# Biases loaded packed instead of multiplied into place, a longer warming burst, and other batches with a copy, in a convolution-attention kernel

## The chip, the cores and the metric

The kernel runs on one core of one Trainium2 chip. Its engines work side by side, each through its own queue in order: TensorE multiplies matrices (PE in the profile, its weight loads PEld), VectorE (DVE), ScalarE (ACT) and GpSimd (POOL) work elementwise, and the queues of SyncE (SP), ScalarE and GpSimd issue transfers (DMA). Matrix products are written to PSUM, which has eight banks of 512 float32 columns; the other engines read them from there.

The metric is the time of one execution on the device in microseconds (us), as the median of several runs.

## The reference

The input `x` has four images of 384 channels and 48 x 48 pixels, so 2304 tokens of 384 channels each, in float32. Cut to what matters:

```python
x_flat = x.reshape(B, C, N).transpose(0, 2, 1)
local = conv_general_dilated(x, conv_w, padding='SAME', feature_group_count=C)   # 7 x 7, each channel alone
inv = bn_gamma * rsqrt(bn_var + BN_EPS)
local = local * inv + (bn_beta - bn_mean * inv)
x_norm = layernorm(x_flat, ln_gamma, ln_beta)          # over the 384 channels
q, k, v = split_heads(x_norm @ qkv_w.T + qkv_b)        # 8 heads of 48
q = q + split_heads(layernorm(local_flat, ln_gamma, ln_beta))
attn = softmax(q @ k.T * 48 ** -0.5)
out = x_flat + (attn @ v) @ proj_w.T + proj_b
```

## The kernel before, in words

**Layout.** The 384 channels lie in three chunks of 128 partitions, packed so that two heads share 128 partitions: 48 channels of one head, 16 of a shared tail, 48 of the next, 16 of the tail (`segments`). Whatever is per channel must come in this order: the convolution's taps, the norms, the biases.

**Tiles.** An image is cut in six groups of 384 tokens for keys and values (`from_x`) and in five query tiles of 8, 10, 10, 10 and 10 pixel rows, 384 or 480 columns each. For each query tile there are eight batches; a batch scores nine blocks of 128 keys against the tile for one pair of heads (`score`, line 1169), ScalarE takes the exponential (lines 1181 and 1185), and the weighted sums follow (`weigh`, line 1206). Tiles are numbered t = 0 to 19 over the four images.

**The convolution** runs on VectorE as a stream of multiply-adds, one for each tap and chunk (line 376). `convolve_first(n)` takes the next n taps of that stream in the start-up, as written by hand; in the attention a planner (`plan`) deals them out to slots (t, s, q), where s is the batch and q a quarter of it: `spare` says how much VectorE time a slot is thought to have, and each tile's taps have a due slot. Since an engine's queue runs in order, taps dealt before a copy or a norm delay it.

**Copies.** A batch scores into pairs of banks. In a batch for which `eased(t, s)` holds, the second half of its third block is copied by VectorE out of PSUM (line 1189) and ScalarE takes its exponential later from there, so that a bank comes free earlier and ScalarE gets time. In image 0 before its last tile, batches 3, 5 and 6 have the copy, and in tile 3 batch 2 too.

**Start-up.** The order is written by hand, and the same on all engines' queues. TensorE first multiplies constant tiles (`warm`, line 1388). The query and key biases come in natural order with one small load on ScalarE's queue (line 202), a few VectorE writes make a matrix of ones that picks rows (`bias_rows`), and four products put the biases in packed order into `qk_vec` (`bias_out`, lines 297 and 301; float32 products count twice in the profile, so eight entries). The first group of x is then normalized in three blocks: mean of the loaded rows (`slab`), centring on VectorE (line 659), squares on ScalarE (line 598), mean of the squares, inverse root (lines 667 to 669 on ScalarE, 678 and 679 on VectorE), scaling (line 736). In between, `pack` (line 251) puts the taps and norms in order, ScalarE copies them out as `vec` (line 258), and scales the weights by the norm's gain (lines 953, 960, 961). `shift_rows` and `columns` (lines 916 and 942) turn the norm's shift into a bias of keys, values and queries, and `key_bias` and `query_bias` add `qk_vec` to it. Then the loop over groups 1 to 5 makes keys, values and queries of each while the next group is normalized (sums on VectorE at lines 608 and 609, their mean on TensorE at line 649), and `convolve_first` fills VectorE between. `products` (line 451) does one chunk of one tile's taps on TensorE instead. The first score follows at line 1169.

Of the kernel before, what the change touches and what calls it, by code (L numbers as in the profile page):

```python
# [16 lines left out]
P = 128  # L17
NH = 8
HD = 48
# [8 lines left out]
SPLIT = 5  # L28
EASED = 2
X_LATER = 3  # L30
WARM = 9
BIASES_AFTER = 2
SHIFTS = 4
AHEAD = 24
SLAB_AT = 40
# [15 lines left out]
def unshifted_pass(  # L51
# [16 lines left out]
    nc = tc.nc  # L68
# [3 lines left out]
    CC = C // P  # L72
    G = RG * W
    NG = N // G
    NB = G // P
    NP = NH // 2
# [5 lines left out]
    NA = len(ROWS)  # L82
# [30 lines left out]
    def two_banks():  # L113
        nonlocal n_banks
        i = n_banks % 8
        n_banks += 2
        return banks[:, i : i + 2, :]
# [4 lines left out]
    def load_packed(dst, src, queue=nc.sync):  # L122
        for p0, piece in segments(src):
            queue.dma_start(out=dst[p0 : p0 + piece.shape[0]], in_=piece)
# [41 lines left out]
    qk_vec = const.tile([P, 2, CC], F32, tag="qk_vec", name="qk_vec")  # L166
    vbp = const.tile([P, CC, 1], F32, tag="vbp", name="vbp")
    pb = const.tile([P, CC], F32, tag="pb", name="pb")
    ident = const.tile([P, P], F32, tag="ident", name="ident")
# [14 lines left out]
    def piece(*shape):  # L184
        nonlocal taken
        size = 1
        for n in shape:
            size *= n
        part = start_up[:, taken : taken + size]
        taken += size  # L190
        names = "abc"[: len(shape)]
        return part.rearrange(
            f"p ({' '.join(names)}) -> p {' '.join(names)}", **dict(zip(names, shape))
        )
# [3 lines left out]

    of_ln = piece(2, CC)
    nc.scalar.dma_start(out=of_ln, in_=ln)  # L200
    biases = piece(2, NP)
    nc.scalar.dma_start(out=biases[0 : 2 * HD], in_=qk_b.rearrange("j d v p -> (j d) v p"))
    of_values = piece(CC, 1)
    nc.scalar.dma_start(out=pb, in_=proj_b)
    staged = [
# [9 lines left out]
    nc.gpsimd.tensor_scalar_add(inv, norms[:, 3], BN_EPS)  # L215
    nc.gpsimd.tensor_tensor(inv, inv, neg_half, ALU.pow)
    load_packed(of_values, v_b.rearrange("o c -> c o"), nc.gpsimd)

    pieces = []
    for c in range(CC):  # L220
        for r, n, first in ((0, HD, 0), (64, HD, 1), (48, 16, 6), (112, 16, 7)):
            head = first + 2 * c if first < 6 else first
            ch = head * HD + (16 * c if first >= 6 else 0)
            while n:
                part = min(n, P - ch % P)
                pieces.append((c, r, ch // P, ch % P, part))
                r, n, ch = r + part, n - part, ch + part
# [48 lines left out]
            load_slab(0, 1, queue=nc.sync)  # L276
    load_packed(w_o, proj_wT)
    loads.close()

    chosen_rows = spread_taps[1][:, 2 * 448 : 2 * 448 + 4 * P].rearrange("p (a m) -> p a m", m=P)  # L280

    def bias_rows():

        rows = chosen_rows.rearrange("p a (j x) -> p a j x", j=2)
        nc.vector.memset(chosen_rows, 0.0)
        nc.vector.tensor_copy(
            rows[:, 0, :, 0:HD], ident[:, 0 : 2 * HD].rearrange("p (j d) -> p j d", j=2)
        )
        nc.vector.tensor_copy(
            rows[:, 1:4, :, HD:64],  # L290
            ident[:, 0 : 2 * HD].rearrange("p (j c r) -> p c j r", j=2, c=CC),
        )

    def bias_out():
        m = two_banks()[:, 0, 0 : 2 * CC].rearrange("p (v c) -> p v c", v=2)
        rows = slice(0, 2 * HD)
        nc.tensor.matmul(
            m, lhsT=chosen_rows[rows, 0, :], rhs=biases[rows, :, 0:CC], start=True, stop=False
        )
        for c in range(CC):  # L300
            nc.tensor.matmul(
                m[:, :, c],
                lhsT=chosen_rows[rows, 1 + c, :],
                rhs=biases[rows, :, CC],
                start=False,
                stop=c == CC - 1,
            )
        nc.scalar.copy(qk_vec, m)

    taps = sorted(range(KS * KS), key=lambda t: (abs(t // KS - PAD), abs(t % KS - PAD)))
    accs = {}
# [148 lines left out]

    def eased(t, s):
        if t < NA - 1:
            return s in (3, 5, 6) or s == 2 and t == NA - 2
        return s > 0 or t >= NA

    def spare(t, s, q):
# [437 lines left out]
    rows = {}  # L907
# [25 lines left out]
                rows[i][:, 288:384].rearrange("o (h u r) -> o u h r", h=2, r=16),  # L933
            )

    def columns():

        r, r2 = two_banks(), two_banks()
        m = {1: r[:, 0, 0:CC], 2: r[:, 1, 0:CC], 0: r2[:, 0, 0:CC]}
        for i in m:  # L940
            for c in range(CC):
                nc.tensor.matmul(
                    m[i][:, c : c + 1],
                    lhsT=row[of_row(i), c * P : (c + 1) * P],
                    rhs=one[of_row(i)],
                    start=True,
                    stop=True,
                )
        return m, r2[:, 1, :G]

    def scale_values(*chunks):
        for c in chunks:
# [425 lines left out]
    def convolve_first(n):  # L1378
        nonlocal n_first
        n_first += n  # L1380
        for _ in range(n):
            next(stream)


    def warm(n):
        m = two_banks()[:, 0, 0:P]
        for _ in range(n):
            nc.tensor.matmul(m, lhsT=mean_w, rhs=ident, start=True, stop=True)

    bias_rows()  # L1390
    in_order_of_channels()
    warm(WARM - BIASES_AFTER)
    bias_out()
    warm(BIASES_AFTER)

    blocks = [slice(i * P, (i + 1) * P) for i in range(NB)]
    raw = slabs[0, 0][0]
# [24 lines left out]
    next(making)  # L1422
    for c in range(CC):
        scale_rows(0, c)
    m, bank = columns()
    convolve_first(11)
    norm = Norm(xn[0, 1])
    norm.mean_by_chunk(norm.src, bank)
    convolve_first(9)
    key_bias(m)  # L1430
    convolve_first(3)
    query_bias(m)
    next(making)
    norm.centre()
    norm.squares()
    both(making)
    convolve_first(5)
    norm.mean_by_chunk(norm.buf)
    norm.root()
    both(making)  # L1440
# [9 lines left out]
    for g in range(1, NG):  # L1450

        last = g == NG - 1
        making = from_x(0, g)
        if last:
            norm.centre()
            norm.squares()
        both(making)
        if not last:
            norm.mean_in_place()
            convolve_first(6)  # L1460
        if g in (3, 5):
            keep_stack(0, g // 2 - 1)
        if last:
            convolve_first(2)
            norm.sum_squares()
            norm.mean_in_place()
            norm.root()
            convolve_first(4)
        else:
            norm.centre()  # L1470
            norm.squares()
        both(making)
        if not last:
            if g == 1:
                taps_out()
            if g == 2:
                products()
                convolve_first(22)
            convolve_first(3 if g == 1 else 5)
            norm.sum_squares()  # L1480
            both(making)
            norm.mean_in_place()
            norm.root()
        if last:
            local_end(0, norm.newton())
            query_end(0, True)
            low_queries(0, 0, nc.gpsimd)
            lows_out(1)
            both(making)
            convolve_first(5)  # L1490
            lows_out(2)
            convolve_first(4)
            both(making)
            convolve_first(6)
            both(making)
            continue
        lows_out(1)
        both(making)
        convolve_first(6)
        lows_out(2)  # L1500
        norm.scale(norm.newton())
        if g == 1:
            taps_spread()
        both(making)
        if g == NG - 2:
            assert n_first >= each
            norm = Norm(accs[0])
            norm.mean_by_chunk(norm.src)
        if g < NG - 2:
            norm = Norm(xn[0, g + 2])  # L1510
            norm.sum()
        convolve_first((7, 5, 6, 6)[g - 1])
    made = n_first - each
    plan(made)
    convolve("start")
# [1 line left out]
    for t in range(NT):  # L1517
        b, g = divmod(t, NA)
        if g == 0 and b:
# [4 lines left out]
            norm = None  # L1524
# [645 lines left out]
```

## Time and profile before

| | us |
|---|---|
| median of three runs | 2699.64 |
| the three runs | 2699.25, 2699.64, 2702.36 |
| the profiled execution's own time | 2702.91 |
| its span, first to last instruction | 2700.4 |
| TensorE busy in it | 2689.2 |
| VectorE busy | 2352.3 |
| ScalarE busy | 1650.4 |
| GpSimd busy | 595.5 |
| first score starts | 152.0 |

A row of the profile names the engine, the line of the kernel, the operation, what it writes and reads, shapes, and how often. In rows in order of time the first two numbers are the start and the length, both in us from the span's first instruction; a bracket says how long the engine was idle before and what ended that. In the chain of waits each row is a stretch of the chain that ended last. Products are pipelined, so a row's length is more than the time from its start to the next row's start; rates are read from starts.

### The profile page before, as it was taken

The page shows a single profiled execution, that of the slowest core. Times are in us where ns is not written, and L with a number is a line of the kernel's source. Part 1 is how long each engine was busy: PE and PEld are TensorE (multiplying, and loading weights), DVE is VectorE, ACT ScalarE, POOL GpSimd, SP SyncE. Part 2 cuts the span into 40 slices and gives each one's busy share as a digit, 9 for nine tenths or more (in the row PEclk, how much of TensorE's full clock was granted, in tenths as well). Part 3 has the DMA queues.
Part 4 walks back from the last instruction along what each step waited for, and adds up shares of the span by engine and source line. Part 5 has one row for each costly group of instructions (what it writes and reads, how often), then busy time and mean ns, then how long its engine had stood idle before and what let it go on. Part 6 is the DMA issues. An engine that isn't in the chain of part 4 may idle for free.

```text
span 2700.4 us, 45544 instructions
## 1 busy us (share of the span) xinstructions
PE 2689.2 (100%) x16444; PEld 1543.1 (57%) x16444; DVE 2352.3 (87%) x4105; ACT 1650.4 (61%) x2489; POOL 595.5 (22%) x1065
## 2 busy tenths in 40 slices
PE   9999999999999999999999999999999999999999
PEld 6565555555566655555555655555555665555555
DVE  8999999999999999888999999888899899887212
ACT  4367667777325777777622767777753376766662
POOL 4441111112462111011155111101116401101110
PEclk9999999999999999999999999999999999999999
DMA  8454443546465545355456553545636644445442
GB/s 175 88 162 136 133 125 115 143 128 159 113 157 162 147 115 146 115 154 136 126 141 159 158 149 110 151 124 140 149 103 166 167 131 132 139 124 147 136 129 94
DMA packets 160251, 370.43 MB, mean 137 GB/s; under 512 B 58400, under 2 KB 107360, under 8 KB 160016
## 3 DMA queue, kind: packets, MB, share of 16 engines
q0 software_dynamic: 70816, 277.78, 36.2%
q1 hardware_dynamic: 83456, 79.29, 13.1%
q10 hardware_dynamic: 5744, 10.36, 1.2%
q8 instruction: 132, 2.16, 0.3%
q14 instruction: 103, 0.84, 0.1%
HBM read 258.14 MB, written 64.14 MB: 119 GB/s over the span
## 4 chain that ended last, share of the span: by engine, by line
PE 89%; DVE 9%; ACT 1%; issue 0%; DMA 0%; DVEq 0%; ACTq 0%
PE banks L1206 38%; PE banks L1169 31%; PE banks L741 19%; DVE acc L376 7%; PE banks L631 0%; DVE qs L1030 0%; DVE acc L659 0%; DVE pt L852 0%; DMA start_up<-in_qk_b_dram 0%; DVE xn L736 0%; DVE pt L1189 0%; DVE xn L659 0%; DVE sq L678 0%; DVE sq L608 0%; DVE sq L609 0%
## 5 line engine op out<-in xcount | busy, mean ns | idle before, releaser
L376 DVE SCALAR_TENSOR_TENSOR acc<-slab,vec,acc 128x470 f32<-128x470 f32 (+10 forms) x2832 | 1657.1, 657 | 0.0
L1206 PE MATMUL banks<-pt,v 128*64 128x480 f32 (+1 forms) x5760 | 1149.7, 553 | 0.0
L1185 ACT ACTIVATE pt<-banks 128x960 f32<-128x960 f32 (+1 forms) x1140 | 1000.6, 948 | 114.7 <-PE banks L1169 59.8
L1169 PE MATMUL banks<-qs,ks 64*128 64x480 f32 (+1 forms) x8640 | 953.0, 372 | 1.5 <-DVE pt L1189 1.4
L1169 PEld LDWEIGHTS banks<-qs,ks 64*128 64x128 f32 x8640 | 786.3, 184 | 222.2 <-issue 113.9
L1206 PEld LDWEIGHTS banks<-pt,v 128*64 128x64 f32 x5760 | 399.8, 137 | 672.4 <-issue 627.0
L813 POOL DMA_DIRECT2D ks<-wide x220 | 159.8, 726 | 1476.8 <-PE banks L1169 1472.5
L1181 ACT ACTIVATE pt<-banks 128x480 f32<-128x480 f32 (+1 forms) x460 | 263.7, 573 | 119.7 <-PE banks L1206 119.2
L741 PE MATMUL banks<-xn,w_qk 128*128 128x384 f32 x864 | 284.0, 486 | 0.0
L741 PEld LDWEIGHTS banks<-xn,w_qk 128*128 128x128 f32 x864 | 164.0, 190 | 114.7 <-issue 0.7
L1189 DVE COPY pt<-banks 128x480 f32<-128x480 f32 (+1 forms) x140 | 89.1, 637 | 151.9 <-PE banks L1169 150.1
L1054 ACT COPY o<-banks 113x480 f32<-113x480 f32 (+1 forms) x80 | 43.6, 545 | 205.4 <-PE banks L1206 205.4
L741 PE MATMUL banks<-w_v,xn 128*128 128x384 f32 x432 | 145.2, 488 | 0.5 <-ACT w_v L953 0.3
L835 ACT COPY v<-banks 128x384 f32<-128x384 f32 x72 | 34.3, 477 | 156.8 <-PE banks L741 156.8
L1064 ACT COPY ao<-banks 113x480 f32<-113x480 f32 (+1 forms) x60 | 32.7, 545 | 151.2 <-PE banks L1206 151.2
L741 PEld LDWEIGHTS banks<-w_v,xn 128*128 128x128 f32 x432 | 81.3, 190 | 59.2 <-DVE xn L736 1.8
L1073 DVE TENSOR_TENSOR ao<-ao,o 113x480 f32<-113x480 f32 (+1 forms) x60 | 37.9, 632 | 59.4 <-ACT o L1054 59.0
L1181 ACT ACTIVATE pt<-pt 128x480 f32<-128x480 f32 (+1 forms) x140 | 88.4, 632 | 0.0
L741 PE MATMUL banks<-af,w_o 128*128 128x384 f32 (+1 forms) x270 | 85.2, 470 | 0.0
L798 POOL DMA_DIRECT2D wide<-pt x120 | 60.1, 504 | 111.5 <-ACT pt L849 106.8
L741 PEld LDWEIGHTS banks<-af,w_o 128*128 128x128 f32 x270 | 51.3, 190 | 31.9
L849 ACT ACTIVATE pt<-banks,qkb 128x384 fp32r<-128x384 f32 x60 | 34.6, 581 | 56.4 <-PE banks L741 51.1
(160 smaller groups left out, 1455.5 us busy)
## 6 DMA issues: line engine op xcount, KB each, us to landing
ks<-wide POOLq DMA_DIRECT2D x220, 768.0 KB, 5.1
qs<-qs SPq DMA_DIRECT2D x346, 60.0 KB
slab<-in_x_dram POOLq DMA_DIRECT2D x22, 432.0 KB, 6.7
wide<-ks POOLq DMA_DIRECT2D x12, 768.0 KB, 5.2
xr<-in_x_dram POOLq DMA_DIRECT2D x16, 576.0 KB, 5.0
rb<-rden SPq DMA_DIRECT2D x32, 270.0 KB
held<-ao POOLq DMA_DIRECT2D x12, 720.0 KB, 4.5
xn<-in_x_dram POOLq DMA_DIRECT2D x36, 216.0 KB, 5.0
```

Of the source, the lines that this page charges most:

```text
L376: nc.vector.scalar_tensor_tensor(dst, src, weight, dst, ALU.mult, ALU.add)
L741: nc.tensor.matmul(dst, lhsT=weights(c), rhs=src(c), start=c == 0, stop=c == CC - 1)
L798: nc.gpsimd.dma_start(out=last[16 * u : 16 * u + 16, 0], in_=k[r : r + 16, 0])
L813: queue.dma_start(out=place_keys(b, p, i), in_=wide[b, p][:, :, at])
L849: nc.scalar.activation(k[:, 0, :], r[:, :G], AF.Identity, bias=bias)
L1054: nc.scalar.copy(part[0 : 64 + HA], sums[0 : 64 + HA, :n])
L1073: nc.vector.tensor_add(dst, dst, part[0 : 64 + HA])
L1169: nc.tensor.matmul(r[:, j, :n], lhsT=ks[rows, w, at], rhs=qs[rows, m, :], start=n_th == 0, stop=n_th == 2,)
L1181: nc.scalar.activation(weights_of[:, at, :n], src, AF.Exp, scale=SCALE)
L1185: nc.scalar.activation(to, r[:, :, :n], AF.Exp, scale=SCALE)
L1189: nc.vector.tensor_copy(weights_of[:, second, :n], r[:, 1, :n])
L1206: nc.tensor.matmul(sums[halves[j], :n], lhsT=values[t // NA, kb // NB][:, first : first + 64], rhs=weights_of[:, at[j], :n], start=start, ...
```

## The change

The query and key biases are no longer loaded in one piece and multiplied into order. Eight small loads on GpSimd's queue, behind the value bias, write them straight into `qk_vec`: for each of queries and keys one load of the 48-channel parts and three of 16-channel tails, with elements of 12 and 4 bytes. The load on ScalarE's queue, `bias_rows` and `bias_out` go. `WARM` rises from 9 products, which stood in two parts (seven, then two behind the bias products), to 12 in one piece.

In the first group, the mean of the second group of x is issued ahead of `columns`, which now gets its banks from outside. VectorE does 17 taps in one go, then centres that group, and adds the key and query biases after that; before, it did 11, 9 and 3 taps around them and centred last. The 11 taps that follow were 5. In the loop two taps leave group 2 (22 to 20), one is added at the end of groups 3 and 4 each (6 to 7), and in the last group 2 and 4 become 1 and 5; the number of taps in the start-up stays at 176.

In image 0 the copy stays in batches 5 and 6 of tiles 0 and 2, in 3 and 5 of tile 1, and in 2, 3, 5 and 6 of tile 3. Batch 3 of tile 0, batch 6 of tile 1 and batch 3 of tile 2 lose it. Since `spare` asks `eased`, the planner deals the taps out a little differently too.

```diff
-WARM = 9
-BIASES_AFTER = 2
+WARM = 12
...
-    biases = piece(2, NP)
-    nc.scalar.dma_start(out=biases[0 : 2 * HD], in_=qk_b.rearrange("j d v p -> (j d) v p"))
...
     load_packed(of_values, v_b.rearrange("o c -> c o"), nc.gpsimd)
+    for j in range(2):
+        r = 64 * j
+        nc.gpsimd.dma_start(out=qk_vec[r : r + HD], in_=qk_b[j, :, :, 0:CC])
+        for c in range(CC):
+            nc.gpsimd.dma_start(
+                out=qk_vec[r + HD : r + 64, :, c], in_=qk_b[j, 16 * c : 16 * c + 16, :, CC]
+            )
...
-    def bias_rows():
...
-    def bias_out():
...
     def eased(t, s):
         if t < NA - 1:
-            return s in (3, 5, 6) or s == 2 and t == NA - 2
+            return s in ((5, 6), (3, 5), (5, 6), (2, 3, 5, 6))[t]
         return s > 0 or t >= NA
...
-    def columns():
-
-        r, r2 = two_banks(), two_banks()
+    def columns(r, r2):
+
...
-        return m, r2[:, 1, :G]
+        return m
...
-    bias_rows()
     in_order_of_channels()
-    warm(WARM - BIASES_AFTER)
-    bias_out()
-    warm(BIASES_AFTER)
+    warm(WARM)
...
-    m, bank = columns()
-    convolve_first(11)
+    r, r2 = two_banks(), two_banks()
     norm = Norm(xn[0, 1])
-    norm.mean_by_chunk(norm.src, bank)
-    convolve_first(9)
+    norm.mean_by_chunk(norm.src, r2[:, 1, :G])
+    m = columns(r, r2)
+    convolve_first(17)
+    norm.centre()
     key_bias(m)
-    convolve_first(3)
     query_bias(m)
     next(making)
-    norm.centre()
     norm.squares()
     both(making)
-    convolve_first(5)
+    convolve_first(11)
...
         if last:
-            convolve_first(2)
+            convolve_first(1)
             norm.sum_squares()
             norm.mean_in_place()
             norm.root()
-            convolve_first(4)
+            convolve_first(5)
...
             if g == 2:
                 products()
-                convolve_first(22)
+                convolve_first(20)
...
-        convolve_first((7, 5, 6, 6)[g - 1])
+        convolve_first((7, 5, 7, 7)[g - 1])
```

More of the change, by code (lines that the diff above doesn't have):

```diff
@@ L278, in unshifted_pass @@
     loads.close()
-    chosen_rows = spread_taps[1][:, 2 * 448 : 2 * 448 + 4 * P].rearrange("p (a m) -> p a m", m=P)
-    def bias_rows():
[L284 to L292, printed above, removed]
-    def bias_out():
[L295 to L308, printed above, removed]
     taps = sorted(range(KS * KS), key=lambda t: (abs(t // KS - PAD), abs(t % KS - PAD)))
```

## The prediction

> **What bounds the kernel now.** I read the page first, then the engines' rows in order of time for the start-up, the chain of waits, and the rows and windows of the attention. The page's shares say that TensorE (PE) hardly rests:
>
> ```profile
> PE 2689.2 (100%) x16444; PEld 1543.1 (57%) x16444; DVE 2352.3 (87%) x4105; ACT 1650.4 (61%) x2489; POOL 595.5 (22%) x1065
> ```
>
> So only two things can shorten the run: PE time that is spent badly, or short waits of PE. The diff touches the start-up (before the first score, at 152.0) and the planner's copies in image 0. PE's first rows (start, length, both us; each float32 product counts as two entries):
>
> ```profile
> 1.81 3.35 PE L1388 MATMUL banks<-ident,mean_w 128*128 128x128 f32 x14 [1.81 <-POOL one L177]
> 6.01 0.56 PE L297 MATMUL banks<-start_up,spread 96*128 96x6 f32 x2 [0.85 <-DMA start_up<-in_qk_b_dram]
> 6.43 1.42 PE L301 MATMUL banks<-start_up,spread 96*128 96x2 f32 x6
> 7.71 1.20 PE L1388 MATMUL banks<-ident,mean_w 128*128 128x128 f32 x4
> 8.70 4.05 PE L741 MATMUL banks<-slab,mean_w 128*128 128x128 f32 x18
> 12.54 1.23 PE L741 MATMUL banks<-sq,mean_w 128*128 128x128 f32 x6
> 13.61 1.66 PE L251 MATMUL banks<-natural,start_up 128*128 128x52 f32 x14
> 15.11 1.57 PE L741 MATMUL banks<-sq,mean_w 128*128 128x128 f32 x12
> 16.51 1.46 PE L741 MATMUL banks<-w_v,xn 128*128 128x384 f32 x4
> 18.24 3.00 PE L741 MATMUL banks<-w_v,xn 128*128 128x384 f32 x8 [0.28 <-ACT w_v L953]
> ```
>
> Equal entries ran at two rates: (12.54 - 8.70) / 18 = 0.213 us each, then (16.51 - 15.11) / 12 = 0.117. The six at 12.54 took 1.07, so the rate doubled among them, at about 13.3. The windows' granted clock reads 1.00 throughout (as in the window's row below, and the same in the first 20 us), so I take the rate from the starts. The warming burst of 3.35 us broke off at the wait for the query and key biases, and the narrow entries after it did not raise the rate.
>
> In the attention of image 0, scoring a batch of 480 columns takes 6.12 us at best (1130.10); here it takes 6.45, and where VectorE (DVE) must copy one half out, up to 333.11 + 2.22 - 328.33 = 7.00:
>
> ```profile
> 174.55 5.38 PE L1169 MATMUL banks<-qs,ks 64*128 64x384 f32 x54
> 185.82 3.60 PE L1169 MATMUL banks<-qs,ks 64*128 64x384 f32 x37
> 190.25 1.84 PE L1169 MATMUL banks<-qs,ks 64*128 64x384 f32 x17 [0.83 <-DVE pt L1189]
> 209.25 5.03 PE L1169 MATMUL banks<-qs,ks 64*128 64x384 f32 x54
> 328.33 4.38 PE L1169 MATMUL banks<-qs,ks 64*128 64x480 f32 x37
> 333.11 2.22 PE L1169 MATMUL banks<-qs,ks 64*128 64x480 f32 x17 [0.40 <-DVE pt L1189]
> 384.68 6.45 PE L1169 MATMUL banks<-qs,ks 64*128 64x480 f32 x54
> 398.45 4.39 PE L1169 MATMUL banks<-qs,ks 64*128 64x480 f32 x37
> 403.04 2.21 PE L1169 MATMUL banks<-qs,ks 64*128 64x480 f32 x17 [0.20 <-DVE pt L1189]
> 1130.10 6.12 PE L1169 MATMUL banks<-qs,ks 64*128 64x480 f32 x54
> ```
>
> The window of tile 1 (us, then busy us and instructions of PE, weight loads, DVE, ACT, POOL, the clock, transfers):
>
> ```profile
> 245.53:357.15 111.62, 111.22 (x731) 60.05 (x729) 110.08 (x180) 78.11 (x104) 13.84 (x21) 1.00 0.47 128
> ```
>
> The three waits are for that copy, which stands in DVE's queue behind convolution taps; DVE is busy 110.08 of 111.62 us in tile 1.
>
> **The change, part by part.**
>
> *Bias products and warming.* Out go the 0.85 us wait, eight narrow entries (6.01 to 7.71) and three short DVE writes that lie in DVE's idle time; in come six more entries of warming. All 24 then run from 1.81 to 1.81 + 24 x 0.213 + 0.16 = 7.1 at the slow rate. The first means need the slab. Its landing has no row: its four loads are issued by 3.04, the nearest rows for landings are 4.0 and 4.8 us, so 7.0 to 7.8, and 8.7 at the latest, since PE did not wait for it then. I take 7.4 instead of 8.70: -1.3.
>
> ```profile
> 1.19 1.85 SPq L124 DMA_DIRECT2D slab<-in_x_dram  x4
> 3.85 2.44 POOL L124 DMA_DIRECT2D start_up<-in_v_b_dram  x4
> 4.70 6.26 SPq L124 DMA_DIRECT2D staged<-in_qkv_wT_dram  x12
> 15.31 0.29 ACT L258 COPY vec<-banks 128x156 f32<-128x156 f32 x1 [0.36 <-PE banks L251]
> ```
>
> ```profile
> xn<-in_x_dram POOLq DMA_DIRECT2D x36, 72.0 KB, 4.8
> start_up<-in_v_b_dram POOLq DMA_DIRECT2D x2, 0.6 KB, 4.0
> ```
>
> *The rate.* In this run a dense burst of 3.35 us was too short, one of 5.6 us (7.71 to 13.3) long enough. So an unbroken one from 1.81 doubles the rate between 5.2 and 7.4. The 38 entries between 8.70 and 15.11 took 6.41 us; at 0.107 (the 14 of L251, 13.61 to 15.11) to 0.117 they take 4.1 to 4.5. I take 4.5, since the third block's square must still be waited for: -1.9. ScalarE's copy of the packed vectors (15.31) and its scalings up to PE's 18.24 then come 3.2 earlier. The value weights are the first four of twelve loads, issued by about 6.8, so landed by 11.6 with 4.8, and wanted at 12.4, behind that copy. Range of both terms together: -1.3 (no doubling) to -3.6 (slab at 7.0).
>
> [...]
>
> *Eight bias loads on GpSimd (POOL).* They queue behind the value bias: issued from 6.3 at 2.44 / 4 = 0.61 each, done at 11.2, landed by about 15.2. The key bias needs them at about 27.6 and POOL's own next work, writing out keys, follows that. Price nothing; one for one, if they landed after 27.6.
>
> *Mean of the second x first; 17 taps in one go.* The number of PE's products stays. Now PE stands 0.80 at 35.41, because DVE does 23 taps before centring; afterwards it does 17, and 15 follow instead of nine.
>
> ```profile
> 35.41 2.20 PE L741 MATMUL banks<-sq,mean_w 128*128 128x384 f32 x6 [0.80 <-ACT sq L598]
> 87.02 0.88 PE L649 MATMUL banks<-sq,mean_w 128*128 128x384 f32 x2 [0.40 <-DVE sq L609]
> 93.95 4.14 PE L741 MATMUL banks<-w_v,xn 128*128 128x384 f32 x12 [0.24 <-DVE xn L736]
> 137.65 0.88 PE L649 MATMUL banks<-sq,mean_w 128*128 128x384 f32 x2 [0.21 <-DVE sq L609]
> 39.43 0.62 DVE L678 SCALAR_TENSOR_TENSOR sq<-banks,eps,sq 128x384 f32<-128x384 f32 x1 [0.33 <-ACT sq L669]
> 130.10 3.75 DVE L376 SCALAR_TENSOR_TENSOR acc<-slab,vec,acc 128x470 f32<-128x470 f32 x6
> 140.29 0.62 DVE L678 SCALAR_TENSOR_TENSOR sq<-banks,eps,sq 128x384 f32<-128x384 f32 x1 [0.34 <-ACT sq L669]
> 135.15 1.17 ACT L598 ACTIVATE sq<-acc 128x1152 f32<-128x1152 f32 x1 [2.90 <-DVE acc L659]
> ```
>
> ```profile
> 44.15 7.96 DVE acc L376 x16
> 73.36 12.45 DVE acc L376 x27
> ```
>
> That frees PE, but the chain of waits (last two rows) is DVE's from 42 to 94, and the number of taps up to there is the same. DVE gains its 0.33 wait at 39.43 and loses some 0.2 waiting for the moved mean: -0.1. I take that, not the 0.8 that PE alone could save; the lower end of this term is -0.8.
>
> *Taps moved.* Two taps leave the 27 before the sums at 87.02: 2 x 12.45 / 27 = -0.9, which PE's waits 0.40 and 0.24 and what hides in its pipeline can use. They come back one each in groups 3 and 4. The last one costs: seven taps of 0.61 (3.75 / 6) instead of six before the centring of the first query tile, and ScalarE's squares (1.17) are covered by one tap instead of two, so the sums at 137.65 come 0.55 later against PE. A fifth tap (0.6) then stands before the query's root is used at 140.29, where 0.34 was waiting: +0.25. Sum up to the first score: -3.2 - 0.1 - 0.9 + 0.55 + 0.25 = -3.4.
>
> *Copies.* Batch 3 of tile 0, batch 6 of tile 1 and batch 3 of tile 2 lose theirs. They then score like neighbours without one: 5.38 instead of 190.25 + 1.84 - 185.82 = 6.27, so -0.89; 6.45 instead of 7.00, -0.55; 6.45 instead of 6.80, -0.35. DVE gets three copies back, 3 x 0.55 to 0.65, about what PE gains, so its load stays where it is:
>
> ```profile
> L1189 DVE COPY pt<-banks x14: 546/648/658, 189.6 to 595.9; 128x480 f32<-128x480 f32 x11, 128x384 f32<-128x384 f32 x3
> ```
>
> The planner's own sums shift single taps between slots of a tile. Where one moves ahead of a copy that stays, up to 0.6 is lost, where one moves behind it, as much is won: 0. Together -1.8 (-2.4 to -0.6).
>
> Total for the profiled execution: -5.2, from 2702.91 (span 2700.4 and 2.5 around it) to **2697.7**.
>
> **How that stands to the median.** The runs shown are 2699.25, 2699.64 and 2702.36; the profiled one lies by the slowest. Two pairs about 3.2 apart, and one thing in the trace is worth 3.2: when the rate doubles. Had the first burst of 3.35 us sufficed, the means would begin at 7.5 and run at the fast rate: -1.2 - 1.9 = -3.1. I read the two lower runs so; they have that gain already and keep 5.2 - 3.1 = 2.1, which leads from their 2699.45 to 2697.4. Both ways meet near **2697.4**, my forecast. Against the median that is -0.08%: no change, as some 0.2% (5.4 us) is what a measurement of this kernel can tell.
>
> **Rivals.** (a) *The two pairs have another cause* than the rate; one profile cannot say. Then the whole 5.2 comes off the median: 2694.4. (b) *The rate still doubles late*: the pause between 7.1 and 7.4 breaks the burst, and it takes 5.6 us from 7.4. Then 1.3 remains of the 3.2: 2702.6 - 3.3 = 2699.3. Against it: the burst is 5.3 us long before the pause. (c) *The copies buy nothing*: DVE, 98.6% busy, gives PE's gain back at the copies that stay (batches 5 and 6 of tile 0, 3 and 5 of tile 1, 5 and 6 of tile 2): 2697.4 + 1.8 = 2699.2. (d) *Slower*, by the same queue: a late copy costs 6.27 - 5.03 (209.25, where it came in time) = 1.2. If DVE comes some 0.8 too late at all six, they cost 7.2, and 2699.2 + 7.2 = 2706.4; two such copies more than eat the gain. It decides from about 0.5 of delay at each; now only the three that go wait.
>
> **How the numbers follow.** Forecast 0.57 (own range 2696 to 2698.6), (a) 0.2, (b) 0.08, (c) 0.11, (d) 0.04. Of (a), which lies near the bound, and of the forecast's edge about 0.17 is faster by over 0.2%; of (d) 0.04 slower; the rest within. The range 2693.9 to 2699.7 holds all but (d) and the tails.
>
> **What would show it.** Right: slab means from about 7.4 at 0.112 each; the vectors' copy near 12.1; first score near 148.6; scoring of the three batches 5.4, 6.45 and 6.45; no wait for L1189's copy over 0.3. Wrong: means still at 0.213; a first score before 148 (PE bound, not DVE) or after 150; waits at the copies that stay; runs of the new kernel that again lie 3 us apart.

## The result, and the profile after

The changed kernel takes 2697.54 us, the median of 20 runs (2696.77 to 2699.66). Twenty runs of the kernel before, the three that the prediction had among them, have a median of 2701.68 (2699.25 to 2704.26), 2.04 above that of those three alone. The ratio is 0.9985, with an interval of 0.9978 to 0.9992: the gain of 4.1 us can be told from none, and with 0.15% it is within the 0.2% that the prediction calls no change. The profiled execution took 2696.89 us with a span of 2695.0; before, 2702.91 and 2700.4. So the span lost 5.4 us.

Lines of the changed kernel have other numbers: 741 is now 712, 649 is 620, 376 is 347, 1169 is 1139, 1189 is 1159, 1388 is 1358, 251 is 255, 258 is 262.

Engines' shares on the page of the changed kernel:

```profile
PE 2686.0 (100%) x16442; PEld 1540.4 (57%) x16442; DVE 2350.0 (87%) x4099; ACT 1650.5 (61%) x2485; POOL 601.3 (22%) x1073
```

TensorE is busy 3.2 us less than before (2689.2), VectorE 2.3 less. TensorE's rows in the start-up, changed kernel, in order of time (start, length, both us; in the bracket the idle time ahead and what ended it):

```profile
1.81 4.47 PE L1358 MATMUL banks<-ident,mean_w 128*128 128x128 f32 x24 [1.81 <-POOL one L176]
7.04 2.25 PE L712 MATMUL banks<-slab,mean_w 128*128 128x128 f32 x18 [0.76 <-DMA slab<-in_x_dram]
9.15 0.94 PE L712 MATMUL banks<-sq,mean_w 128*128 128x128 f32 x6
...
11.42 1.57 PE L712 MATMUL banks<-sq,mean_w 128*128 128x128 f32 x12
...
30.76 2.10 PE L712 MATMUL banks<-sq,mean_w 128*128 128x384 f32 x6
...
82.29 0.81 PE L620 MATMUL banks<-sq,mean_w 128*128 128x384 f32 x2
...
88.78 4.14 PE L712 MATMUL banks<-w_v,xn 128*128 128x384 f32 x12
...
133.10 0.88 PE L620 MATMUL banks<-sq,mean_w 128*128 128x384 f32 x2 [0.83 <-DVE sq L580]
...
147.45 3.82 PE L1139 MATMUL banks<-qs,ks 64*128 64x384 f32 x40
```

The 24 entries of warming take 4.47 us, less than 24 at the slow rate, so the rate doubled inside the burst: with n slow entries, 0.213 n + 0.117 (24 - n) + 0.16 = 4.47 gives n = 15.6, so at about 5.1. The slab's landing is a wait now (0.76), and its means run at (9.15 - 7.04) / 18 = 0.117 each. The waits at the mean of squares (35.41 before, 30.76 now) and at 87.02 are gone; the one at the last sums grew from 0.21 to 0.83. The first score comes 152.0 - 147.45 = 4.55 earlier.

One stretch of the chain of waits, the copy of the packed vectors, and the first use of the biases (changed kernel):

```profile
39.98 7.97 DVE acc L347 x16
```

```profile
11.62 0.29 ACT L262 COPY vec<-banks 128x156 f32<-128x156 f32 x1 [0.25 <-PE banks L255]
```

```profile
26.97 0.15 DVE L934 TENSOR_TENSOR qkb<-qk_vec,banks 128x3 f32<-128x3 f32 x1
```

The attention of image 0 hardly moved. The windows of tile 2 and the sum over tiles 0 to 3, changed kernel (us, then busy us and instructions of PE, weight loads, DVE, ACT, POOL, the clock, transfers):

```profile
351.92:464.02 112.10, 111.51 (x730) 59.80 (x728) 110.23 (x181) 78.10 (x103) 13.85 (x21) 1.00 0.47 127
...
sum 427.04, PE 426.32 PEld 237.48 DVE 413.06 ACT 301.38 POOL 66.20; mean PE 106.58 PEld 59.37 DVE 103.27 ACT 75.34 POOL 16.55
```

The same sum before:

```profile
sum 427.49, PE 425.96 PEld 238.01 DVE 413.33 ACT 301.44 POOL 66.42; mean PE 106.49 PEld 59.50 DVE 103.33 ACT 75.36 POOL 16.61
```

That is 0.45 us less, where 1.8 was forecast (tiles 0 to 2 alone: 317.13 before, 316.57 now). Tile 2 even takes 112.10 instead of 111.98 with one copy less. VectorE, busy 110.23 there, is as full as before (110.04). Scoring, batch by batch, shows where. Changed kernel:

```profile
181.22 5.36 PE L1139 MATMUL banks<-qs,ks 64*128 64x384 f32 x54
...
203.75 5.56 PE L1139 MATMUL banks<-qs,ks 64*128 64x384 f32 x54
216.00 5.45 PE L1139 MATMUL banks<-qs,ks 64*128 64x384 f32 x54
...
323.68 6.44 PE L1139 MATMUL banks<-qs,ks 64*128 64x480 f32 x54
...
393.21 6.43 PE L1139 MATMUL banks<-qs,ks 64*128 64x480 f32 x54
...
420.74 4.39 PE L1139 MATMUL banks<-qs,ks 64*128 64x480 f32 x37
425.71 2.22 PE L1139 MATMUL banks<-qs,ks 64*128 64x480 f32 x17 [0.59 <-DVE pt L1159]
...
436.07 6.14 PE L1139 MATMUL banks<-qs,ks 64*128 64x480 f32 x54
```

And before:

```profile
220.97 5.06 PE L1169 MATMUL banks<-qs,ks 64*128 64x384 f32 x54
...
426.34 6.14 PE L1169 MATMUL banks<-qs,ks 64*128 64x480 f32 x54
440.61 6.70 PE L1169 MATMUL banks<-qs,ks 64*128 64x480 f32 x54
```

The three batches that lost their copy (181.22, 323.68, 393.21) score in 5.36, 6.44 and 6.43, as forecast. But batches 5 and 6 of tile 0, which keep it, now take 5.56 and 5.45 instead of 5.03 and 5.06, and batch 5 of tile 2 takes 425.71 + 2.22 - 420.74 = 7.19 instead of 6.14, behind a copy that comes late. One batch that keeps its copy wins: batch 6 of tile 2, whose copy came late before (6.70), scores in 6.14 now. From one first score to the next, the lengths of the three that lose are 12.25, 13.75 and 15.33, before 11.72, 13.36 and 14.27; that of the one that wins is 14.27, before 14.83. These lengths are what the expectations below call a batch's time.

### The profile page after: what moved, and what is told of

It reads as the page before. It is cut to its first block, busy times and chain, and to the rows that moved or that the text cites. A ratio compares the mean times of both kernels' runs of the same rounds, so it can differ in the third digit from the quotient of the medians.

```text
span 2695.0 us, 45539 instructions
## 1 busy us (share of the span) xinstructions
PE 2686.0 (100%) x16442; PEld 1540.4 (57%) x16442; DVE 2350.0 (87%) x4099; ACT 1650.5 (61%) x2485; POOL 601.3 (22%) x1073
## 4 chain that ended last, share of the span: by engine, by line
PE 96%; DMA 1%; DVE 1%; ACT 0%; issue 0%; SPq 0%; POOL 0%; DVEq 0%; ACTq 0%
PE banks L1176 42%; PE banks L1139 35%; PE banks L712 19%; DVE acc L347 1%; DMA xn<-in_x_dram 1%; PE banks L422 0%; DMA slab<-in_x_dram 0%; PE banks L602 0%; DMA staged<-in_qkv_wT_dram 0%; PE banks L620 0%; ACT pt L1155 0%; DMA qs<-qs 0%; DVE xn L707 0%; ACT sq L569 0%; DMA wide<-pt 0%
```

## The experiments

Each was timed beside the kernel before on the same chip. Four chips were used; the median of the kernel before lay between 2701.65 and 2702.19 on them. Diffs are cut to what matters.

**Warming alone.** The kernel before, with 12 products of warming in one burst and the bias products behind it:

```diff
-WARM = 9
-BIASES_AFTER = 2
+WARM = 12
...
-    warm(WARM - BIASES_AFTER)
+    warm(WARM)
     bias_out()
-    warm(BIASES_AFTER)
```

> The kernel before, with one edit: all 12 warming products in one burst, and the bias products behind them. If the unbroken burst is what counts: the rate of PE doubles before the slab's means, which start at about 7.9 (the burst ends near 6.2, then eight narrow entries at 0.11) and run at 0.112 each; first score 2.5 to 3 us before 152.0; the runs lie within about 1.5 us of each other. If the eight narrow products and the wait for the biases are what counts: they are still there, the first score moves by less than 1 us, and the runs spread over 3 to 5 us as those of the kernel before.

Measured: 2700.41 (ratio 0.9996, 0.9986 to 1.0005). Its rows:

```profile
1.81 4.97 PE L1387 MATMUL banks<-ident,mean_w 128*128 128x128 f32 x24 [1.81 <-POOL one L176]
6.61 0.28 PE L296 MATMUL banks<-start_up,spread 96*128 96x6 f32 x2
6.76 0.81 PE L300 MATMUL banks<-start_up,spread 96*128 96x2 f32 x6
7.43 2.25 PE L740 MATMUL banks<-slab,mean_w 128*128 128x128 f32 x18
...
148.91 1.31 PE L1168 MATMUL banks<-qs,ks 64*128 64x384 f32 x12
```

The means run at 0.117 from 7.43, and the first score is 3.1 earlier, the size that the prediction gave to the rate and the burst together. The median is only 1.5 below that of the kernel before, and the runs spread over 2.5, which neither expectation had. Behind the burst the bias products cost 0.82 us; only the 0.39 by which 7.43 lies behind 7.04 is won by loading the biases packed.

**A short burst.** The changed kernel with `WARM = 7`:

> The changed kernel with 7 warming products instead of 12, as many as stood ahead of the wait before; PE idles from about 5 until the slab lands at 7.0. If a burst of 3.35 us is too short in most runs: the means start at 7.0 at 0.213 each, the rate doubles at 10 to 14, first score 1.5 to 2.5 us later than the changed kernel's 147.45, and the runs spread by 3 us or more. If the loading in place of products brings the gain: first score near 147.5 and the same time and spread as the changed kernel (2697.5, most within 1 us).

Measured: 2698.83 (0.9988, 0.9979 to 0.9998), runs from 2696.8 to 2699.73, the first score of the profiled one at 150.04, 2.6 later than in the changed kernel.

```profile
1.81 3.35 PE L1358 MATMUL banks<-ident,mean_w 128*128 128x128 f32 x14 [1.81 <-POOL one L176]
6.99 4.18 PE L712 MATMUL banks<-slab,mean_w 128*128 128x128 f32 x18 [1.83 <-DMA slab<-in_x_dram]
10.96 1.49 PE L712 MATMUL banks<-sq,mean_w 128*128 128x128 f32 x6
```

PE idles 1.83 us and all 18 means run at (10.96 - 6.99) / 18 = 0.22: the slow rate again. So what counts in these profiles is the length of the unbroken burst, not that the bias products left. Three of the ten runs lie below 2697.7, as eleven of the changed kernel's twenty do, and seven above 2698.6; the profiled one is the slowest of them.

**Copies alone.** The kernel before with the new `eased`:

> The kernel before with the new choice of batches with a copy alone (and the planner's rooms that follow it). If PE's gain is kept: tiles 0 to 2 take 317.1 - 1.8 = 315.3 us from first score to first score of tile 3. If VectorE gives it back at the copies that stay, as in the changed kernel's trace: 316.4 to 317.1, with batch 5 or 6 of tile 0 and batch 5 of tile 2 0.3 to 1.1 us longer than before; the start-up as before (first score at 152 where the rate doubles late, at 149 where it doubles early).

Measured: 2699.38 (0.9993, 0.9984 to 1.0003). Windows of tiles 0 to 2, summed:

```profile
sum 316.42, PE 315.82 PEld 177.51 DVE 310.18 ACT 221.80 POOL 51.16; mean PE 105.27 PEld 59.17 DVE 103.39 ACT 73.93 POOL 17.05
```

Before, they took 93.53 + 111.62 + 111.98 = 317.13: a gain of 0.7, lost in part in tile 3. The same copies are late as in the changed kernel (12.05, 13.74, 15.34), with a start-up that was not touched. The giving back belongs to the choice of copies and the taps that the planner moved with it. The median is 2.6 below that of the kernel before, more than these windows explain; the runs fall in two groups of five, 2698.34 to 2698.97 and 2699.80 to 2701.10, so the median hangs on how many fall in each (see the two pairs below).

**Order and taps alone.** The kernel before with the moved mean and the moved taps:

> The kernel before with the new order of the second mean, the columns and the taps alone. By the prediction's sum: -0.1 - 0.9 + 0.55 + 0.25 = -0.2 at the first score against a start with the rate doubling at the same place, so 151.8 if it comes at 13.4 as in the profile of before; the wait ahead of 35.41 is gone, that at 87.02 too, that at 137.65 grows from 0.21 to 0.8. If PE and not VectorE sets the pace: -0.8 to -1.5. The changed kernel's trace shows -4.55 in all at the first score against -3.69 at the vectors' copy, which would leave -0.9 to this part.

Measured: 2701.16 (0.9998, 0.9988 to 1.0008).

```profile
8.68 3.10 PE L741 MATMUL banks<-slab,mean_w 128*128 128x128 f32 x18
11.61 0.83 PE L741 MATMUL banks<-sq,mean_w 128*128 128x128 f32 x6
12.28 1.66 PE L251 MATMUL banks<-natural,start_up 128*128 128x52 f32 x14
...
149.98 2.21 PE L1168 MATMUL banks<-qs,ks 64*128 64x384 f32 x22
```

Here the broken burst did a little better: the means took (11.61 - 8.68) / 18 = 0.163, and the packing started at 12.28 instead of 13.61. Of the 2.0 us by which the first score is earlier, 1.33 is that; 0.7 is left for order and taps.

**Old rooms.** The changed kernel, but the planner's room follows the old choice (`roomed` is the old `eased`):

```diff
-            time -= 0.5 * (s % 2 == 0) + 0.5 * eased(t, s)
+            time -= 0.5 * (s % 2 == 0) + 0.5 * roomed(t, s)
```

> The changed kernel with its new choice of batches with a copy, but the planner reckons the room for taps by the old choice (3, 5, 6, and 2 in tile 3). Theory 1: the copies that stay come late because the planner moved single taps ahead of them. Then batches 5 and 6 of tile 0 go back from 12.25 and 13.75 us to the 11.72 and 13.36 of the kernel before, batch 5 of tile 2 from 15.33 to 14.27, while the batches without a copy keep 11.25 and 13.76, so tiles 0 to 2 together fall from 316.57 to about 315.2 us and the time by 1.3 to 1.8. Theory 2: VectorE's load as a whole gives the gain back, wherever the single taps stand: tiles 0 to 2 stay within 0.4 of 316.57 and the time within 0.5.

Measured: 2696.54 (0.9985, 0.9976 to 0.9994).

```profile
203.81 5.56 PE L1144 MATMUL banks<-qs,ks 64*128 64x384 f32 x54
216.06 5.07 PE L1144 MATMUL banks<-qs,ks 64*128 64x384 f32 x54
...
420.60 6.10 PE L1144 MATMUL banks<-qs,ks 64*128 64x480 f32 x54
```

Half and half. Batch 6 of tile 0 and batch 5 of tile 2 are back at 5.07 and 6.10: there a tap that the planner had moved stood ahead of the copy. Batch 5 of tile 0 stays at 5.56. Batch 6 of tile 2 is back at 14.81 too, so the planner's shift had won there. Tiles 0 to 2 take 315.82 instead of 316.57, about half of the 1.4 that theory 1 wanted there; the median is 1.0 below the changed kernel's.

**Old copies.** The changed kernel with the old `eased`:

> The changed kernel with the old choice of batches with a copy, so the changes of the start-up alone. If start-up and copies are independent, the first score stays at 147.45 within 0.6, tiles 0 to 2 take 317.1 us as before instead of 316.57, and the time is 0.5 above the changed kernel's. If the copies' gain is only eaten by the moved work of the start-up, tiles 0 to 2 stay at 316.6 and the time is the same.

Measured: 2698.98 (0.9991, 0.9982 to 1.0), first score at 147.63. Windows of tiles 0 to 2, summed:

```profile
sum 317.39, PE 315.79 PEld 178.88 DVE 310.64 ACT 222.39 POOL 50.95; mean PE 105.26 PEld 59.63 DVE 103.55 ACT 74.13 POOL 16.98
```

The start-up's gain stands without the copies, and the copies are worth 317.39 - 316.57 = 0.8 in these tiles. The median stands 1.4 above the changed kernel's, where 0.5 was expected; the two profiles differ by 0.18 at the first score, 0.82 in these tiles and 0.17 in tile 3.

**Last taps.** The changed kernel with the tap of group 4 back in group 3, and 2 and 4 in the last group:

```diff
-        convolve_first((7, 5, 7, 7)[g - 1])
+        convolve_first((7, 5, 8, 6)[g - 1])
```

> The changed kernel, but the tap that was moved to the end of group 4 stands in group 3 (7, 5, 8, 6), and the last group has 2 taps ahead of the sums and 4 behind, as before. Theory 1, the sum's terms of +0.55 and +0.25: the wait ahead of the sums' mean at 133.10 falls from 0.83 to about 0.2, the wait for the query's root is as in the kernel before, the first score comes 0.5 to 0.8 earlier than 147.45, and the time falls by as much. Theory 2, VectorE's chain sets the end: the tap only moves, and the first score stays within 0.2.

Measured: 2697.44 (0.9987, 0.9978 to 0.9996), first score at 147.08.

```profile
132.72 0.88 PE L620 MATMUL banks<-sq,mean_w 128*128 128x384 f32 x2 [0.36 <-DVE sq L580]
```

The wait fell from 0.83 to 0.36, so by 0.47. The first score moved by 0.37, from a start that was 0.09 later (VectorE's chain of 16 taps at 39.98, in the changed kernel at 39.89): the wait is paid one for one. In the median the gain can't be seen.

**One tap behind the copy.** Old rooms, last taps, and one tap of slot 3 of batch 4 moved to slot 0 of batch 5, in tile 0:

```diff
+        share["slot", 0, 4, 3] -= 1
+        share["slot", 0, 5, 0] += 1
```

> The changed kernel with the planner's rooms by the old choice and the last groups' taps as in the two runs before (7, 5, 8, 6; 2 and 4), and one tap of tile 0 that stood ahead of the copy in batch 5 now stands behind it. Theory: batch 5 of tile 0 is late because VectorE enters it one tap behind after batch 3 went faster than VectorE, so one tap less ahead is enough: batch 5 goes from 12.25 us to 11.7, batch 6 keeps 13.37, tile 0 takes 92.6, the first score stands at 147.1 as with those taps alone, and the time is about 2695.7 to 2696.2. Rival: what VectorE can't do ahead of batch 5 it does ahead of batch 6: batch 6 goes from 13.37 to 13.75 or more and tile 0 stays within 0.3 of 93.1; the time is then 2696.2 to 2696.6.

Measured: 2696.76 (0.9981, 0.9972 to 0.999).

```profile
19.86 2.33 PE L894 MATMUL banks<-staged,vec 128*1 128x384 f32 x18 [1.85 <-DMA staged<-in_qkv_wT_dram]
...
205.87 5.06 PE L1146 MATMUL banks<-qs,ks 64*128 64x384 f32 x54
217.62 5.18 PE L1146 MATMUL banks<-qs,ks 64*128 64x384 f32 x54
```

Batch 5 scores in 5.06 again, batch 6 gives back 0.1, and tile 0 takes 92.70, near the 92.6 of the theory. All of the copies' gain is there now: 317.13 - 315.38 = 1.75 in tiles 0 to 2 (and again in the run with late loads, which has the same copies and taps there: 315.31). VectorE is as full as in the changed kernel there, busy 98.0% in both. But the first score stood at 149.59, since in this execution the weights landed at 19.7 and PE waited 1.85 for them. The forecast time was missed by half a microsecond, and by the medians it can't be told from the kernel with old rooms (2696.54).

**One tap ahead of each copy.** Old rooms, and at each of the six copies one tap moved from slot 0 of its batch to slot 3 of the batch ahead:

> The changed kernel with the planner's rooms by the old choice, and at each of the six copies that stay in tiles 0 to 2 one tap is moved from behind the copy to ahead of it: the delay of some 0.6 us (0.5 at 384 columns) that the prediction's slower case speaks of. By the price in that case, 0.4 for each of the first 0.5 us late and all of it from there, tiles 0 to 2 take between 2 and 6 us more than the 315.82 of the kernel without the move, and the time rises by as much. Rival: a copy has slack of a tap wherever it is not late yet, so only those that are at their edge (batches 5 of tile 0 and tile 2) lose, 0.5 to 1.1 each, together 1 to 2 us.

Measured: 2698.91 (0.9989, 0.998 to 0.9999).

```profile
1.81 4.29 PE L1368 MATMUL banks<-ident,mean_w 128*128 128x128 f32 x24 [1.81 <-POOL one L176]
...
204.37 3.59 PE L1149 MATMUL banks<-qs,ks 64*128 64x384 f32 x37
208.72 1.84 PE L1149 MATMUL banks<-qs,ks 64*128 64x384 f32 x17 [0.76 <-DVE pt L1169]
...
283.07 4.39 PE L1149 MATMUL banks<-qs,ks 64*128 64x480 f32 x37
287.65 2.22 PE L1149 MATMUL banks<-qs,ks 64*128 64x480 f32 x17 [0.18 <-DVE pt L1169]
```

Tiles 0 to 2 take 317.58, so 1.76 more for six taps, and the time is 2.4 above that of the kernel with old rooms. Three batches pay, 0.63, 0.63 and 0.53 (5 of tile 0, 3 of tile 1, 5 of tile 2); the other three take as long as without the move. The rival holds, with tile 1's batch 3 on the edge too.

**Old taps.** The changed kernel with the old copies and the old taps of the loop:

> The changed kernel with the old choice of copies and the old taps of the loop (22 in group 2; 7, 5, 6, 6; 2 and 4 in the last): warming, loads and the moved mean are left. By the prediction's terms the moved taps gain 0.9 at the sums of 82.29 and give 0.8 back by the first score: the sums come at about 83.2 and the first score stays within 0.2 of the 147.63 with the moved taps. Rival, from the places in the changed kernel's trace: the taps gained 0.56 at the sums and gave back only 0.18, so the sums come at about 82.9 and the first score at about 148.0. If TensorE and not VectorE sets the end, the taps gain nothing and both stay at 82.3 and 147.6.

Measured: 2699.41 (0.9991, 0.9981 to 1.0001), first score at 148.62. The chain's 16 taps (39.89 in VectorE's rows of the changed kernel) start at 40.46 here and at 40.07 with the old copies alone, so both are counted from there. Sums in the two, old taps first:

```profile
83.43 0.88 PE L620 MATMUL banks<-sq,mean_w 128*128 128x384 f32 x2 [0.42 <-DVE sq L580]
```

```profile
82.46 0.81 PE L620 MATMUL banks<-sq,mean_w 128*128 128x384 f32 x2
```

The moved taps win (83.43 - 40.46) - (82.46 - 40.07) = 0.58 at the sums, as the rival had it. At the products of line 712 behind them (90.57 and 88.95) they are worth 1.23, as a wait of 0.45 goes there too; of that 0.63 is given back by the first score, where (148.62 - 40.46) - (147.63 - 40.07) = 0.60 is left. The prediction's terms had next to nothing left, the rival 0.4.

**Bias loads twice.** The changed kernel with eight more loads of the same, into a tile that nothing reads:

```diff
+    for to in (twice, qk_vec):
```

> The changed kernel, but the eight small bias loads are done twice, first into a tile that nothing reads: sixteen loads on GpSimd's queue between the weights' loads. Theory, from the one profile in which the last of the weights landed at 19.7 us and TensorE waited 1.85 for it: small loads share the way of the weights at 0.2 to 0.4 us each, and the cover (landing 16.7, wanted at 17.5 in the changed kernel) is 0.8 us. Then the weights land at 18.3 to 20, TensorE waits 1 to 2.5 us ahead of the products of weights and norms, the first score comes as much later than 147.45, and the time rises by 1 to 2.5. Rival, the prediction's price of nothing: small loads fit in gaps, the weights land within 0.5 of 16.7, and the time stays within 0.5; the biases themselves land by 23, ahead of the 26.97 at which they are wanted.

Measured: 2697.69 (0.9984, 0.9975 to 0.9994). TensorE's rows, and one of GpSimd's queue:

```profile
1.81 5.49 PE L1360 MATMUL banks<-ident,mean_w 128*128 128x128 f32 x24 [1.81 <-POOL one L176]
7.11 2.36 PE L714 MATMUL banks<-slab,mean_w 128*128 128x128 f32 x18
...
17.66 2.11 PE L889 MATMUL banks<-staged,vec 128*1 128x384 f32 x18
```

```profile
10.67 0.50 POOL L221 DMA_DIRECT2D twice<-in_qk_b_dram  x1 [0.81 <-DMA start_up<-in_v_b_dram]
```

No wait for the weights at 17.66 (in the changed kernel the last of them landed at 16.69, and the same products start at 17.49), and no change of time. The theory of a shared way fell. Among the issues on GpSimd's queue from the ninth load on, eight rows show a wait for an earlier load, 0.23 to 0.81 us: three for loads of the value bias (0.81 in the row), then five for the added ones. In the changed kernel the ninth to twelfth load were issued 0.28 to 0.29 us after the load eight before had landed (at 8.43, 9.13, 10.17 and 10.96). With these waits the sixteen spread out, the last two issued from 17.51, and VectorE, which uses the biases at 27.15, still does not wait for them.

**Bias loads late.** The kernel with the tap behind the copy, with the loads held until the last weights landed:

```diff
+    late = const.tile([P, 1], F32, tag="late", name="late")
+    nc.gpsimd.tensor_copy(late, staged[0][:, CC - 1, 0:1])
```

> The kernel with the tap behind the copy, but GpSimd issues the eight bias loads only once the last of the weights has landed (it copies one element of them first). Theory that the small loads delay the weights: the weights land by 16, TensorE never waits for them, the runs lie closer together than 2695.4 to 2698.3, and the median falls from 2696.76 to about 2695.5. Rival: the loads now stand in the way of the rows of the second group of x, or come after 26.97 themselves; then a wait of 0.5 to 2 us stands ahead of that group's mean or of the bias columns, and the time is as before or up to 1.5 longer.

Measured: 2699.64 (0.9989, 0.998 to 0.9998), runs from 2694.88 to 2702.54.

```profile
31.48 0.16 DVE L943 TENSOR_TENSOR qkb<-qk_vec,banks 128x3 f32<-128x3 f32 x1 [4.33 <-DMA qk_vec<-in_qk_b_dram]
```

Issued from 16.88, the biases keep VectorE waiting 4.33, until 31.48. The first score comes at 151.49, 4.4 later than with the same taps and early loads (147.08): one for one. The rival holds and is worse than it said. Its fastest run is the fastest of all runs here, so the wait can't be as long in every execution. The weights had landed by 16.35, when GpSimd's copy of the last of them starts, at least 0.3 earlier than in the changed kernel (16.69); but in the kernel before, without these loads, they landed at 16.62, so a cost of the small loads to the weights is not shown.

## Why the prediction came out right, and where its steps did not

The median of 2697.54 lies at the forecast 2697.4 partly by luck, since errors cancelled: the start-up gave 1.15 more than its sum, the copies 1.35 less, the end 0.48 that no term had. For the profiled execution -5.2 was forecast; the span lost 5.4, the execution's own time 6.0.

*Slab means and rate, -3.2 forecast, -3.69 measured* (copy of the vectors at 11.62 instead of 15.31). The slab's means began at 7.04, not 7.4: -1.66 for -1.3. The 38 entries took 11.42 - 7.04 = 4.38, forecast 4.5: -2.03 for -1.9. The rate behaved as written, and rival (b), a late doubling, fell with it. The 5.6 us that sufficed in the kernel before count from 7.71; but the narrow entries ahead of them came without a pause from 6.01, so it may as well have been 7.3. Warming alone and the short burst show it from both sides.

*Order, -0.1 forecast, -0.48 measured.* The chain's 16 taps start at 39.98 instead of 44.15, which is 4.17, of which 3.69 came from ahead. The wait of 0.33 at 39.43 went, as forecast. The step that failed is "loses some 0.2 waiting for the moved mean": there was no such wait here. (With the tap behind the copy, where TensorE stood 1.85 us for the weights, the chain's 16 taps start at 42.50 in VectorE's rows, 2.61 later than in the changed kernel (39.89), of which 0.46 came from the slab.) In the run with order and taps alone the same difference is 1.82 - 1.33 = 0.49 (its taps start at 42.24, before 44.06). That VectorE and not TensorE sets this stretch held: TensorE's 0.80 at 35.41 went, and 0.48 came of it. The sign "a first score before 148 (PE bound, not DVE)" was badly set: 147.45 came from four terms.

*Taps.* 93.95 became 88.78, so 5.17, which is 1.00 past the 4.17: forecast 0.9. The wait at the last sums grew by 0.62: forecast 0.55. The run with old taps has 1.23 and 0.63 for the two. *The fifth tap ahead of the query's root, +0.25,* cost nothing: -5.17 + 0.62 = -4.55 is already the whole of the first score. Together -4.55 against -3.4.

*Copies, -1.8 forecast, -0.45 measured.* The three gains came in full. The step that failed is "where one moves ahead of a copy that stays, up to 0.6 is lost, where one moves behind it, as much is won: 0". They did not cancel: three batches lost 0.53, 0.39 and 1.06 (more than the 0.6 allowed), one won 0.56. That one had a late copy before, which "now only the three that go wait" passes over; the other copies that stay came in time already, and had little to win. The run with old rooms shows that the planner's shift cost 0.75 in all; the run with one tap behind the copy, that batch 5 of tile 0 was late because VectorE reached it one tap behind, TensorE having won 0.89 in batch 3 and VectorE a copy of 0.55 (that last reason is argued, not tried). This is rival (c) in its place, the copies that stay, and in amount 1.35 of its 1.8; its reason, a VectorE too full, does not hold, since the tap behind the copy brings back the whole gain with VectorE as full. Rival (d) has the place right and the price too high: 1.76 for six delays of a tap (0.5 to 0.6 us), not the 7.2 for 0.8, because only copies at the edge pay.

*The end.* The last write of VectorE to the end of the span took 0.48 less than before (2690.47 + 0.52 to 2695.0, against 2695.39 + 0.52 to 2700.4). Nothing in the change touches it; one profile each can't say more.

*Bias loads at nothing.* Held: wanted at 26.97, landed by 17.3 (forecast 15.2). The price past that, one for one, is shown by the late loads.

*The two pairs.* The kernel before does run at two times. Of its 126 runs beside the changed kernel and the experiments, 36 lie between 2699.16 and 2700.39, 90 between 2701.12 and 2704.26, and none between; the medians of the two groups are 2.6 apart, where the prediction had 3.2. The three other kernels with a broken or short burst (copies alone, order and taps alone, the short burst) leave a gap of 0.8 to 1.4 among their runs too. All four such profiles are of runs in the upper group, and in all four the rate doubles late. The changed kernel has 18 of 20 runs within 1.5 us. All this fits the reading that the first burst suffices in some runs, but it is not shown, since no run of a lower group was profiled. Two things speak against it as the only cause: warming alone, with the rate doubled early in its profile, spread over 2.5 without a gap, and the old taps, with an unbroken burst, have a gap of 0.85. So rival (a) is not refuted as to the cause. Its 2694.4 counted from a median of three that lay 2 us too low; from the median of 20 the same 5.2 leads to 2696.5. What else spreads the runs stays open; late weights, as with the tap behind the copy, are one candidate.

The reading of the two pairs assumes that the place of the doubling varies, and between the profiles it does. Bursts of 3.35 or 3.36 us failed in four of them (the kernel before, copies alone, order and taps alone, the short burst), yet 24 entries of warming took 4.29 us in one (one tap ahead), which by the sum used for the changed kernel puts the doubling at 4.7, so 2.9 us into the burst; in another (loads twice) they took 5.49, and the slab means behind them 2.36 instead of 2.25, so that it came at about 7.3, 5.5 us in. What sets the place is not shown.

## What to carry to other kernels

Where products start at about half the rate, as here (0.213 us an entry, then 0.117), give TensorE one unbroken burst that lasts until the rate has doubled. A wait of 0.85 us within it left the first 38 entries 2.0 us slower (6.41 instead of 4.38), while a wait of 1.16 us behind the doubling (one tap ahead) did not bring the slow rate back: the means behind it ran at (9.37 - 7.26) / 18 = 0.117. Taking work off an engine that keeps the others waiting gains only if what it does next is not late for them: price each deadline that stays, and look which of them have slack, instead of adding up the moved work to zero. A median of three from a kernel whose runs spread over 5 us, in two groups, can be off by 2; make the sum against the profiled execution as well.

## What the runs showed of the hardware beyond that

With the broken or short burst the rate doubled after 10 us (by the starts of the rows, at about 10.5 among the means in order and taps alone, between about 12.7 and 13.3 behind them in the other three); with unbroken ones of 24 entries between about 4.7 and 7.3, though these programs begin alike. The same twelve weight loads did not land alike: the last of them was down at 16.62 in the kernel before, at 16.69 in the changed one, by 16.35 with late loads, and at 19.7 with the tap behind the copy. There the 18 entries that need it took 2.33 us, and so they did with one tap ahead and with old taps, where they start about 0.1 behind the end of the row ahead (17.88 and 17.82); in all other profiles they took 2.11 and did not wait. These three profiles are of the three runs timed on one of the chips. And small loads of 4 to 12 bytes an element, issued from 16.88 to 20.7, kept VectorE waiting until 31.48, where those issued from 6.28 to 11.24 were down by 17.34.
